# A graph and mixture-of-experts block on one core: second norm and router moved into the attention's steps, one shared-expert chunk moved behind the experts, expert weights requested behind the token table

## The chip, the cores and the metric

The kernel runs on one NeuronCore of one Trainium2 chip. The core has a matrix engine (TensorE, PE in the profile; its weight loads are PEld), a vector engine (VectorE, DVE), an activation engine (ScalarE, ACT), GpSimd (POOL) and a sync engine (SP) that issues DMAs; ACT and POOL can issue DMAs too. Each engine works through its own stream of instructions in order and waits for the others on semaphores. The metric is the device time of one execution in microseconds (us), the median of several runs.

## The reference, cut to what matters

The input is a graph of 1250 nodes with 512 features and 21250 edges. Four layers follow each other, each added to its input and each fed with a layer norm of it:

```python
x = x + attention(norm(x), edges)        # 8 heads of 32; exp(q.k), weighted by edge counts, normalised
                                         # per receiver; two 512-wide layers with relu; x_norm + out
x = x + moe(norm(x))                     # router: softmax over 64 experts, top 6; capacity 234 tokens;
                                         # gated experts of 256; plus 2 shared experts / 2
x = x + messages(norm(x), edges, attr)   # per edge relu([h[src], attr] W1 + b1) W2 + b2, summed per node,
                                         # a GRU cell, batch norm; h + bn
x = x + kan(norm(x))                     # two layers of cubic splines and silu
```

In the second layer each token goes to its six best experts. Its place inside an expert is its rank among the tokens that chose that expert, in token order; a token whose rank is 234 or more is dropped there. So routing a tile of tokens needs the counts of all tiles before it, and the first expert can start only when every token has been placed.

## The kernel before

Nodes are padded to 1280 and lie in `NT` = 10 tiles of 128 (`xr` keeps their features on chip, `hT` the normed features transposed). Wide matmuls go by `CHUNKS` of 512, 512 and 256 nodes: tiles 0 to 3, 4 to 7, 8 and 9. Everything is float32 but for masks. The program is unrolled. A planner puts the instructions of each engine in order: earlier lines of the program go first where two are ready by its own estimate; `tc.issue_after(ins)` holds a block's instructions behind `ins` on the same engine. A pool of tiles that takes over the memory of a closed pool waits for that whole pool, unless it was opened with `reuse_waits="tile"`, when each tile waits for those alone whose place it takes.

Stages, with times of the profiled execution:

- *Norm, projections and edge counts* (to 166 us).
- *Attention's steps* (166 to 385 us). There are 60 steps: 3 chunks of receivers, 2 halves of the heads, 10 tiles of senders. `scores` (L348) makes two PSUM tiles `ps` of two banks each, out of three that rotate; ACT turns them into `ex` (L358), DVE into `wt` (L360); `weighted` (L366) multiplies two steps later. `normalised` closes a half, `output` (L386) a chunk: its two dense layers are emitted in the middle of the next chunk's first half, and behind the steps for the last chunk. [...]
- *Second norm, routing and shared experts* (385 to 560 us). `layernorm` (L139) over all ten tiles, with the normed rows written to the table `xtab` in DRAM by POOL; then routing in two groups of `RG` = 5 tiles (L493 to L558): logits, softmax, the six best, one-hot `hot`, its sum `sel`, the counts before each token through two small matmuls (`pc`), the copy `slot`, the place `tat`, and 30 scatters by POOL of (token, weight) pairs into the table `tokt`. Behind it the experts are ranked by load (L566 to L591), and the shared experts run over the three chunks (L594 to L633): hidden layer `pg`, `pu`, `g`, `sT`, then `py` added into `xr`. In the last chunk SP reads the table back (`tokb`, L608) and two matmuls sort it into `tok`, `gate` and `goal`. Weights of router, shared experts and W1 came by ACT's queue long before.
- *Experts* (560 to 1085 us). 64 experts, 28 of them with two parts of 128 and 112 rows. `load` (L645) has SP request 1.5 MB of weights into one of four buffers; `rows` gathers tokens from `xtab` by POOL; `result` adds weighted rows by POOL into one of two accumulators `acc` in DRAM. The first four loads wait for nothing but the ranking.
- *Behind the experts* (1085 to 1168 us). The 20 parts of `acc` are read and added to `xr` (L742 to L746), the third norm runs in groups of two tiles, each tile is multiplied by W1 (L765) and stored in the table `ptab` (L769).
- *Messages, GRU, splines* (to the end). POOL gathers rows of `ptab` per edge, so it starts when all of the table is stored.

Of the kernel before, what the change touches and what calls it, by code (L numbers as in the profile page):

```python
# [74 lines left out]
def gnn_ffn_kernel(ctx: ExitStack, tc: tile.TileContext, a: dict, out: bass.AP):  # L75
# [63 lines left out]
    def layernorm(work, psum, each=None, pt_bufs=None, group=NT, residual=False):  # L139


        st = small.tile([P, NT, 6], F32, name="st")
        mv = small.tile([P, NT, 2], F32, name="mv")
        rs = small.tile([P, NT], F32, name="rs")
        for t0 in range(0, NT, group):
            ts = slice(t0, t0 + group)
            for t in range(t0, t0 + group):
                nc.vector.bn_stats(st[:, t], xr[:, t])
                nc.vector.bn_aggr(mv[:, t], st[:, t])
            nc.vector.tensor_scalar(rs[:, ts], mv[:, ts, 1], EPS, None, op0=OP.add)  # L150
            nc.scalar.activation(rs[:, ts], rs[:, ts], AF.Sqrt)
            nc.vector.reciprocal(rs[:, ts], rs[:, ts])
            for t in range(t0, t0 + group):
                h = work.tile([P, D], F32, name="h")
                nc.vector.tensor_scalar(h, xr[:, t], mv[:, t, 0:1], rs[:, t:t + 1],
                                        op0=OP.subtract, op1=OP.mult)
                if each:
                    each(t, h)
                pt = psum.tile([P, DC, P], F32, name="pt", bufs=pt_bufs)
                for c in range(DC):  # L160
                    nc.tensor.transpose(pt[:, c], h[:, c * P:(c + 1) * P], ident)  # L161
                nc.scalar.activation(hT[:, :, t * P:(t + 1) * P], pt, AF.Copy)
        if residual:
            up = small.tile([P, NT], F32, name="up")
            nc.vector.tensor_scalar(up, rs, 1.0, None, op0=OP.add)
            down = small.tile([P, NT], F32, name="down")
            nc.vector.tensor_mul(down, rs, mv[:, :, 0])
            for t in range(NT):
                nc.vector.tensor_scalar(xr[:, t], xr[:, t], up[:, t:t + 1], down[:, t:t + 1],
                                        op0=OP.mult, op1=OP.subtract)  # L170
# [6 lines left out]

    until_moe = ExitStack()
    shared = until_moe.enter_context(tc.tile_pool(name="shared", bufs=1))
    rw = shared.tile([P, DC, NE], F32, name="rw")  # L180
    rb = shared.tile([P, NE], F32, name="rb")
    sg = shared.tile([P, 2, DC, 2 * FF], F32, name="sg")
    sd = shared.tile([P, 2 * FF // P, D], F32, name="sd")
# [5 lines left out]
    zero = shared.tile([P, D], F32, name="zero")  # L189
# [4 lines left out]
    with tc.tile_pool(name="gat", bufs=1) as gw:  # L194
# [13 lines left out]
        with tc.tile_pool(name="gat_a", bufs=3) as work, \  # L208
# [9 lines left out]
            st = keep.tile([P, NT, 6], F32, name="st")  # L218
            mv = keep.tile([P, NT, 2], F32, name="mv")
            rs = keep.tile([P, NT], F32, name="rs")  # L220
            down = keep.tile([P, NT], F32, name="down")
            up = keep.tile([P, NT], F32, name="up")

            def norm(t0):

                ts = slice(t0, t0 + 2)
                for t in range(t0, t0 + 2):
                    nc.vector.bn_stats(st[:, t], xr[:, t])
                    nc.vector.bn_aggr(mv[:, t], st[:, t])
                nc.vector.tensor_scalar(rs[:, ts], mv[:, ts, 1], EPS, None, op0=OP.add)  # L230
                nc.scalar.activation(rs[:, ts], rs[:, ts], AF.Sqrt)
                nc.vector.reciprocal(rs[:, ts], rs[:, ts])
                nc.vector.scalar_tensor_tensor(down[:, ts], mv[:, ts, 0], -1.0, rs[:, ts], op0=OP.mult,
                                               op1=OP.mult)
                nc.vector.tensor_scalar(up[:, ts], rs[:, ts], 1.0, None, op0=OP.add)
                for t in range(t0, t0 + 2):
                    h = work.tile([P, D], F32, name="h", bufs=2)
                    nc.scalar.activation(h, xr[:, t], AF.Identity, bias=down[:, t:t + 1],
                                         scale=rs[:, t:t + 1])
                    pt = psum.tile([P, DC, P], F32, name="pt")  # L240
                    for c in range(DC):
                        nc.tensor.transpose(pt[:, c], h[:, c * P:(c + 1) * P], ident)
                    nc.scalar.activation(hT[:, :, t * P:(t + 1) * P], pt, AF.Copy)
                    nc.scalar.activation(xr[:, t], xr[:, t], AF.Identity, bias=down[:, t:t + 1],
                                         scale=up[:, t:t + 1])
# [20 lines left out]
            for n0, n in CHUNKS:  # L266
                others += [lambda t=t: norm(t) for t in range(n0 // P, (n0 + n) // P, 2)]
# [6 lines left out]
            for b in range(NT):  # L274
# [20 lines left out]
                if b in (3, 4, 5, 6):  # L295
                    with tc.issue_after(cc.ins):
                        if b == 3:
                            nc.scalar.dma_start(out=rw, in_=a["router"].rearrange("(c p) e -> p c e", p=P))
                            nc.scalar.dma_start(out=rb, in_=row(R_RB, NE))
                        elif b < 6:  # L300
                            nc.scalar.dma_start(out=sg[:, b - 4],
                                                in_=a["shared_in"][b - 4].rearrange("(c p) f -> p c f", p=P))
                        else:
                            nc.scalar.dma_start(out=sd, in_=a["shared_out"].rearrange("(c p) d -> p c d", p=P))
# [37 lines left out]

        with tc.tile_pool(name="gat_e", bufs=3) as work, \
                tc.tile_pool(name="gat_o", bufs=2) as owork, \
                tc.tile_pool(name="gat_s", bufs=3, space=PSUM) as psum, \
# [63 lines left out]
            ready, done, acc, aggT = [], None, None, None  # L409
            for i in range(len(steps) + 2):  # L410
# [10 lines left out]
                if b == NT // 2 and half == 0 and done:  # L421
                    output(*done)
                    done = None
                if b == NT - 1:
# [3 lines left out]
            output(*done)  # L428


    until_edges = ExitStack()
    mgw = until_edges.enter_context(tc.tile_pool(name="msg_w", bufs=1, side="right"))
    w1 = mgw.tile([P, DC, D], F32, name="w1")
    nc.scalar.dma_start(out=w1, in_=a["W1"][:D].rearrange("(c p) f -> p c f", p=P))
    b1 = mgw.tile([P, D], F32, name="b1")
    nc.scalar.dma_start(out=b1, in_=row(R_B1, D))


    with tc.tile_pool(name="moe", bufs=1) as mw, tc.tile_pool(name="moe_w", bufs=4) as ew:
        tri = mw.tile([P, P], BF, name="tri")  # L440
        nc.gpsimd.affine_select(out=tri, in_=ones, pattern=[[1, P]], base=0, channel_multiplier=-1,
                                compare_op=OP.is_gt, fill=0.0)
        onesb = mw.tile([P, P], BF, name="onesb")
        nc.vector.memset(onesb, 1.0)
        ei = mw.tile([P, NE], I32, name="ei")
# [760 lines left out]
```

## Time and profile before

| | |
|---|---|
| median of 3 runs | 2061.09 us (2058.55 to 2063.27) |
| profiled execution, its own time | 2108.56 us |
| its span | 2106.7 us |
| mean granted TensorE clock | 0.959 |
| TensorE busy | 1920.8 us, 91% |
| VectorE busy | 1036.7 us, 49% |
| ScalarE busy | 722.7 us, 34% |
| GpSimd busy | 468.1 us, 22% |
| DMA | 250.56 MB, mean 119 GB/s |

The profile is one execution. A row of the order of time gives the start, the time taken, the engine, the line, the operation with the tile it writes and those it reads, how many were merged, and in square brackets how long the engine had been idle before it and what ended that wait. A row of stretches gives the busy time of each engine in a part of the span. "issue" and "remote" mark waits that the recorded semaphores don't explain. The profiled execution took 47.5 us longer than the median.

### The profile page before, as it was taken

The page shows a single profiled execution, that of the slowest core. Times are in us where ns is not written, and L with a number is a line of the kernel's source. Part 1 is how long each engine was busy: PE and PEld are TensorE (multiplying, and loading weights), DVE is VectorE, ACT ScalarE, POOL GpSimd, SP SyncE. Part 2 cuts the span into 40 slices and gives each one's busy share as a digit, 9 for nine tenths or more (in the row PEclk, how much of TensorE's full clock was granted, in tenths as well). Part 3 has the DMA queues.
Part 4 walks back from the last instruction along what each step waited for, and adds up shares of the span by engine and source line. Part 5 has one row for each costly group of instructions (what it writes and reads, how often), then busy time and mean ns, then how long its engine had stood idle before and what let it go on. Part 6 is the DMA issues. An engine that isn't in the chain of part 4 may idle for free. (4 is left out here: it accounts for less than half of the span.)

```text
span 2106.7 us, 20943 instructions
## 1 busy us (share of the span) xinstructions
PE 1920.8 (91%) x7761; PEld 1033.7 (49%) x7761; DVE 1036.7 (49%) x1690; ACT 722.7 (34%) x1114; POOL 468.1 (22%) x436
## 2 busy tenths in 40 slices
PE   6999999784999999999957899999999968889889
PEld 4573224441666666666523233333444756465454
DVE  8667786550211111111125455551122269999995
ACT  3216554200022121121211234341112178777773
POOL 0000000165144444444420556650000000000000
PEclk9999999896999999999988999999999988999999
DMA  6010000231299999999972677770100020000000
GB/s 234 24 40 2 1 1 1 75 98 26 59 280 272 279 280 272 274 269 276 281 225 84 210 234 240 245 238 16 53 23 0 1 90 1 1 10 11 10 1 19
DMA packets 68945, 250.56 MB, mean 119 GB/s; under 512 B 11760, under 2 KB 14448, under 8 KB 59860
## 3 DMA queue, kind: packets, MB, share of 16 engines
q1 hardware_dynamic: 24658, 137.60, 18.7%
q0 software_dynamic: 36240, 92.89, 17.3%
q10 hardware_dynamic: 7922, 18.50, 2.6%
q8 instruction: 67, 1.10, 0.2%
q14 instruction: 58, 0.48, 0.1%
HBM read 211.98 MB, written 36.96 MB: 118 GB/s over the span
## 5 line engine op out<-in xcount | busy, mean ns | idle before, releaser
L718 POOL DMA_INDIRECT acc<-y,goal x92 | 144.5, 1570 | 215.2 <-ACT y L716 120.4
L173 POOL DMA_INDIRECT hg<-ptab,srci x167 | 158.4, 949 | 144.0 <-DVE m L802 53.9
L1069 PE MATMUL pk<-basis,w1s 128*128 128x256 f32 x640 | 158.6, 401 | 29.6 <-DVE basis L1051 29.6
L800 PE MATMUL pm<-w1e,eat 128*128 128x512 f32 x334 | 169.7, 623 | 6.5 <-DVE m L802 5.6
L713 PE MATMUL py<-w,gT 128*128 128x512 f32 x368 | 169.5, 595 | 2.0 <-ACT gT L706 1.4
L1091 PE MATMUL py<-w2s,basis 128*128 128x512 f32 x320 | 148.0, 626 | 21.2 <-DVE basis L1051 21.2
L1069 PEld LDWEIGHTS pk<-basis,w1s 128*128 128x128 f32 x640 | 124.1, 199 | 64.8 <-DVE basis L1051 46.1
L802 DVE TENSOR_TENSOR m<-pm,hg 128x1024 f32<-128x1024 f32 x84 | 102.3, 1218 | 103.6 <-PE pm L800 83.2
L803 ACT ACTIVATE m<-m 128x1024 f32<-128x1024 f32 x84 | 88.3, 1051 | 164.7 <-DVE m L802 148.8
L1028 DVE SCALAR_TENSOR_TENSOR cube<-held,knots,sq 128x512 f32<-128x512 f32 x180 | 136.0, 757 | 1.7 <-ACT sq L1024 1.7
L716 ACT ACTIVATE y<-py,gate 128x512 f32<-128x512 f32 (+1 forms) x92 | 63.3, 688 | 206.5 <-PE py L713 197.7
L1024 ACT ACTIVATE sq<-held,negk 128x512 f32<-128x512 f32 x180 | 126.1, 710 | 20.6 <-DVE held L1016 20.6
L360 DVE SCALAR_TENSOR_TENSOR wt<-ex,cnts 128x1024 f32<-128x1024 f32 (+1 forms) x120 | 118.7, 1039 | 23.0 <-ACT ex L358 22.9
L693 PE MATMUL pg<-w,xT 128*128 128x512 f32 x288 | 129.5, 592 | 0.2 <-issue 0.2
L358 ACT ACTIVATE ex<-ps 128x1024 f32<-128x1024 f32 (+1 forms) x120 | 100.6, 881 | 77.3 <-PE ps L353 64.6
L173 POOL DMA_INDIRECT xg<-xtab,tok x92 | 90.2, 981 | 127.6 <-PE pt L689 44.4
L1091 PEld LDWEIGHTS py<-w2s,basis 128*128 128x128 f32 x320 | 64.0, 201 | 103.4 <-issue 76.8
L800 PEld LDWEIGHTS pm<-w1e,eat 128*128 128x128 f32 x334 | 55.5, 190 | 102.6 <-issue 89.6
L682 DVE TENSOR_TENSOR gT<-gx,pu 128x480 f32<-128x480 f32 x28 | 18.3, 654 | 177.0 <-PE pu L679 177.0
L713 PEld LDWEIGHTS py<-w,gT 128*128 128x128 f32 x368 | 65.6, 186 | 76.0 <-issue 71.9
L679 PE MATMUL pg<-xT,w 128*128 128x240 f32 x448 | 98.1, 372 | 2.9
L697 DVE TENSOR_TENSOR gs<-gs,pg 128x256 f32<-128x256 f32 x36 | 15.2, 422 | 168.6 <-ACT gs L696 168.6
(273 smaller groups left out, 3076.3 us busy)
## 6 DMA issues: line engine op xcount, KB each, us to landing
w<-in_experts SPq DMA_DIRECT2D x64, 1536.0 KB
eat<-in_edge SPq DMA_DIRECT2D x20, 512.0 KB
acc<-zero SPq DMA_DIRECT2D x22, 256.0 KB
part<-acc SPq DMA_DIRECT2D x20, 256.0 KB
w1s<-in_w1s ACTq DMA_DIRECT2D x4, 1024.0 KB
w2s<-in_w2s SPq DMA_DIRECT2D x2, 2048.0 KB
wih<-in_Wih ACTq DMA_DIRECT2D x4, 768.0 KB
whh<-in_Whh ACTq DMA_DIRECT2D x4, 768.0 KB
```

Source lines behind the costliest of these rows:

```text
L173: nc.gpsimd.indirect_dma_start(out=dst, out_offset=None, in_=table, in_offset=IndirectOffsetOnAxis(ap=at, axis=0))
L358: nc.scalar.activation(ex[:, :, :n], p[:, :, :n], AF.Exp, scale=DK ** -0.5)
L360: nc.vector.scalar_tensor_tensor(wt[:, :, :n], ex[:, :, :n], HUGE, cnts[:, b, None, n0:n0 + n].to_broadcast([P, 2, n]), op0=OP.min, op1=OP ...
L693: nc.tensor.matmul(ph[:m], xT[:, c, :m], self.w[:, c:2 * DC:DC], start=c == 0, stop=c == DC - 1)
L713: nc.tensor.matmul(py[:m], self.gT[:, f, at:at + m], self.w[:, k:k + 2].rearrange("p a b -> p (a b)"), start=f == 0, stop=f == 1)
L718: nc.gpsimd.indirect_dma_start(out=next(turn), out_offset=IndirectOffsetOnAxis(ap=goal[:m, self.r, h:h + 1], axis=0), in_=y[:m, j], in_off ...
L800: nc.tensor.matmul(pm[:, i], eat_t, w1e, start=True, stop=True)
L802: nc.vector.tensor_add(m[:, :k], pm[:, :k], hg[:, :k])
L1024: nc.scalar.activation(self.sq[k], self.x, AF.Square, bias=negk[:, k:k + 1])
L1028: nc.vector.scalar_tensor_tensor(self.cube[k], self.x, knots[:, k:k + 1], self.sq.pop(k), op0=OP.subtract, op1=OP.mult)
L1069: nc.tensor.matmul(pk[o], w[:, o * P:(o + 1) * P], b[:, c], start=half == 0 and g == 8 and c == 0, stop=half == 1 and g == 7 and c == 1)
L1091: nc.tensor.matmul(py[m], b[:, c, m * P:(m + 1) * P], w, start=g == 8 and c == 0, stop=g == 7 and c == 1)
```

## The change

Seven edits belong together.

1. The two norms in the code become one class `Norm`, whose `parts` is a generator: it yields behind each two tiles of statistics and behind each tile. ACT can make `h` (`scalar=True`) and did so in the first norm already.
2. Routing becomes a generator `route(t0, n, ...)`, defined ahead of the attention. Its constants are made there. It runs by chunk: tiles 0 to 3, 4 to 7, 8 and 9. Behind a chunk's `output`, each following step of the attention emits one part; what is left runs behind the last step. Its PSUM tiles are `ps` tiles of the scores.
3. Router weights stay where they were in time; the shared experts' weights are requested by SP behind the attention's steps, into memory that the attention's tiles leave (`reuse_waits="tile"`), no longer by ACT in the count stage.
4. The shared experts become a function. Chunk 0 runs ahead of the table, chunk 2 behind it, chunk 1 behind the experts.
5. The first expert's weights are held behind the request for `tokb` (`loads` starts with it).
6. W1 and `b1` are requested behind the tenth expert's weights by SP, no longer by ACT ahead of the routing.
7. Behind the experts, pools wait by tile; parts, third norm, W1 and stores go by pairs of tiles in the order 0, 2, 8, 4, 6, with the third norm's residual update last. `rT` is cleared by DVE, no longer by POOL.

```diff
@@ Norm
-    def layernorm(work, psum, each=None, pt_bufs=None, group=NT, residual=False):
+    class Norm:
+        def parts(self, t0, n, work, psum, name="pt", each=None, scalar=False, bufs=None, pt_bufs=None):
...
+                if (t - t0) % 2:
+                    yield
...
+                if scalar:
+                    nc.scalar.activation(h, xr[:, t], AF.Identity, bias=self.down[:, t:t + 1],
+                                         scale=rs[:, t:t + 1])
...
+                yield
@@ count stage
-                if b in (3, 4, 5, 6):
+                if b == 3:
...
-                            nc.scalar.dma_start(out=sg[:, b - 4],
-                                                in_=a["shared_in"][b - 4].rearrange("(c p) f -> p c f", p=P))
@@ routing, ahead of the attention's steps
+        def route(t0, n, work, psum):
+            yield from norm2.parts(t0, n, work, psum, name="ps", scalar=True, bufs=2, each=lambda t, h: nc.gpsimd.dma_start(
+                out=xtab[1 + t * P:1 + (t + 1) * P], in_=h))
...
+            pl = psum.tile([P, n, NE], F32, name="ps")
...
+            nc.scalar.activation(pr, pr, AF.Exp)
+            yield
...
+            with nc.allow_low_precision(reason="zeros and ones"):
+                nc.vector.tensor_reduce(sel[:, ts], hot.rearrange("p t k e -> p t e k"), AX.X, OP.add)
+            yield
+            pc = psum.tile([P, n, NE], F32, name="ps")
...
+            slot, u = new("slot", NE), new("u", NE)
+            nc.vector.tensor_copy(slot, pc)
...
@@ attention's steps
-            ready, done, acc, aggT = [], None, None, None
+            ready, done, acc, aggT, parts = [], None, None, None, iter(())
...
                 if b == NT // 2 and half == 0 and done:
                     output(*done)
+                    parts = chain(parts, route(done[0] // P, done[1] // P, rwork, psum))
                     done = None
+                else:
+                    next(parts, None)
...
             output(*done)
+            for _ in chain(parts, route(done[0] // P, done[1] // P, rwork, psum)):
+                pass
@@ shared experts' weights
+    shared = until_moe.enter_context(tc.tile_pool(name="shared", bufs=1, reuse_waits="tile"))
...
+    for i in range(2):
+        nc.sync.dma_start(out=sg[:, i], in_=a["shared_in"][i].rearrange("(c p) f -> p c f", p=P))
+    nc.sync.dma_start(out=sd, in_=a["shared_out"].rearrange("(c p) d -> p c d", p=P))
@@ table and shared experts
-            for n0, n in CHUNKS:
-                sT = keep.tile([P, 2 * FF // P, 512], F32, name="sT")
...
+            last = shared_experts(*CHUNKS[0], keep, psum, psum1)
+            tokb = keep.tile([P, P, 2], F32, name="tokb")
+            landed = nc.sync.dma_start(out=tokb, in_=tokt[:NPOS].rearrange("(q p) o -> q p o", p=P))
...
+            shared_experts(*CHUNKS[2], keep, psum, psum1)
-            loads, turn = [], cycle(accs)
+            loads, turn = [landed], cycle(accs)
...
-                        with tc.issue_after(loads[-1].ins) if i else nullcontext():
+                        with tc.issue_after(loads[-1].ins) if loads else nullcontext():
                             experts[i].load()
...
+            with tc.issue_after(loads[10].ins):
+                nc.sync.dma_start(out=w1, in_=a["W1"][:D].rearrange("(c p) f -> p c f", p=P))
+                nc.sync.dma_start(out=b1, in_=row(R_B1, D))
@@ behind the experts
+    psum = finishing.enter_context(tc.tile_pool(name="msg_p", bufs=2, space=PSUM))
+    psum1 = finishing.enter_context(tc.tile_pool(name="msg_q", bufs=1, space=PSUM))
+    shared_experts(*CHUNKS[1], late, psum1, psum1)
+    norm3 = Norm()
+    for t0 in (0, 2, 8, 4, 6):
+        for t in (t0, t0 + 1):
+            for i, acc in enumerate(accs):
+                part = ywork.tile([P, D], F32, name=f"part{i}")
+                nc.sync.dma_start(out=part, in_=acc[t * P:(t + 1) * P])
+                nc.vector.tensor_add(xr[:, t], xr[:, t], part)
+        norm3.group(t0, 2, lwork, psum)
+        for t in (t0, t0 + 1):
+            pp = psum.tile([P, D], F32, name="pp")
...
+            nc.sync.dma_start(out=ptab[t * P:(t + 1) * P], in_=pv)
+    norm3.residual(0, NT)
...
-            nc.gpsimd.memset(rT, 0.0)
+            nc.vector.memset(rT, 0.0)
```

The new function for the shared experts, called with `psum` of two buffers ahead of the experts and with `psum1` of one buffer for both behind them:

```python
    def shared_experts(n0, n, work, psum, psum1):
        sT = work.tile([P, 2 * FF // P, 512], F32, name="sT")
        for f in range(2 * FF // P):
            pg = psum.tile([P, 512], F32, name="pg")
            pu = psum1.tile([P, 512], F32, name="pu")
            for i, p in ((0, pg), (1, pu)):
                for c in range(DC):
                    nc.tensor.matmul(p[:, :n], sg[:, i, c, f * P:(f + 1) * P], hT[:, c, n0:n0 + n],
                                     start=c == 0, stop=c == DC - 1)
            g = work.tile([P, 512], F32, name="g", bufs=2)
            nc.scalar.activation(g[:, :n], pg[:, :n], AF.Silu)
            nc.vector.tensor_mul(sT[:, f, :n], g[:, :n], pu[:, :n])
        for t in range(n // P):
            po = psum.tile([P, D], F32, name="py")
            for f in range(2 * FF // P):
                last = nc.tensor.matmul(po, sT[:, f, t * P:(t + 1) * P], sd[:, f], start=f == 0,
                                        stop=f == 2 * FF // P - 1)
            xs = xr[:, n0 // P + t]
            nc.vector.scalar_tensor_tensor(xs, po, 0.5, xs, op0=OP.mult, op1=OP.add)
        return last
```

## The prediction

> **What bounds the kernel now.** I read the page first, then the busy time by stretches, then the order of time around the widest holes of TensorE.
>
> The page's busy row; the busy time by stretches (columns: stretch, length, busy PE, PEld, DVE, ACT, POOL, granted clock, DMA share, GB/s):
>
> ```profile
> PE 1920.8 (91%) x7761; PEld 1033.7 (49%) x7761; DVE 1036.7 (49%) x1690; ACT 722.7 (34%) x1114; POOL 468.1 (22%) x436
> ...
> 271.40:325.65 54.25, 51.69 (x481) 14.82 (x480) 49.60 (x51) 34.33 (x44) 0.00 (x0) 1.00 0.00 1
> 325.65:346.80 21.15, 21.15 (x52) 8.87 (x48) 4.98 (x8) 2.94 (x5) 0.00 (x0) 1.00 0.00 1
> 346.80:370.40 23.60, 23.08 (x321) 10.19 (x320) 21.02 (x33) 14.26 (x27) 0.00 (x0) 1.00 0.01 2
> ...
> 385.20:559.90 174.70, 131.52 (x422) 73.01 (x423) 60.36 (x151) 19.74 (x30) 72.20 (x79) 0.84 0.22 65
> 559.90:1085.20 525.30, 520.24 (x1993) 338.53 (x1991) 90.13 (x157) 102.46 (x191) 229.25 (x179) 1.00 0.91 266
> 1085.20:1168.30 83.10, 44.96 (x129) 22.29 (x129) 43.52 (x93) 8.65 (x19) 10.77 (x7) 0.78 0.40 128
> ```
>
> TensorE sets the pace nearly everywhere, so the change is worth what it takes out of TensorE's holes: 43 us of 174.7 between the attention and the experts, 38 of 83.1 behind the experts. But in the attention's steps VectorE is almost as full: 49.6 of 54.25, 21.0 of 23.6. The order of time shows the holes:
>
> ```profile
> 392.02 3.65 PE L161 MATMUL pt<-ident,h 128*128 128x128 f32 x16 [6.83 <-DVE h L155]
> ...
> 512.10 6.24 PE L601 MATMUL pu<-hT,sg 128*128 128x512 f32 x8 [28.38 <-issue]
> ...
> 1116.87 3.80 PE L161 MATMUL pt<-ident,h 128*128 128x128 f32 x16 [31.71 <-DVE h L155]
> ...
> 489.58 0.60 ACT L604 ACTIVATE g<-pg 128x512 f32<-128x512 f32 x1 [27.27 <-remote]
> ...
> 511.35 0.69 DVE L605 TENSOR_TENSOR sT<-g,pu 128x512 f32<-128x512 f32 x1 [37.87 <-issue]
> ...
> 509.33 0.96 POOL L553 DMA_INDIRECT tokt<-entry,tat  x1 [0.30 <-issue]
> ...
> 513.14 0.33 SPq L608 DMA_DIRECT2D tokb<-tokt  x1
> ```
>
> The hole at 484 to 512 is odd: the matmuls that ACT and DVE want were issued 21 us and more before, no dependence is late, and it began with four weight transfers (456 to 478, DMA share 0.94) and ended with the scatters. Lost by it: 5.0 us at 468, 28.4 at 484, and 3.3 and 2.8 in two groups that took 6.75 and 6.24 us instead of 3.43: 39.6. Without it the table (requested at 513.1, some 2.5 us to land) would hold up TensorE by 2.5, so 37 us are at stake.
>
> [...]
>
> **The change, part by part.**
> 1. *Routing in the attention (tiles 0 to 3, 4 to 7).* A group of five costs DVE: `sel` 3.46; `hot`, `hu`, `pos` 2.16, 2.16, 2.14; eight passes over 320 elements at 0.49; max and index 2.3; `before` 1.1; small ones. For four tiles, 4/5 of what goes by elements: 2.8 + 5.2 + 3.1 + 1.7 + 0.9 + 2.0 small = 15.6 us (the statistics ran in the steps before, too). Tiles 0 to 3 fall into 271.4 to 325.65: 49.6 + 15.6 = 65.2 against 54.25: +11. Tiles 4 to 7 fall into 346.8 to 370.4: 21.0 + 15.6 = 36.6 against 23.6, +13, of which the last two parts (1.7 and 2.4) come behind the last `wt`: +9. TensorE's share (transposes 4 x 0.43, router 32 at 0.12 to 0.19, counting 0.5: some 6 a group) and ACT's (`h` and `hT` 8 x 0.6, two table switches) lie beside that. ACT's square root and exponential wait for DVE with the next steps' `ex` queued behind them, and TensorE's `weighted` matmuls wait for those through `wt`; the lookahead of two steps (5.9 or 3.3 us) should cover that. POOL has nothing else in these steps, so its 8 table writes and 48 scatters there delay nobody. The routing's 12 `ps` tiles come out of the three that the scores rotate in: 5 us for bubbles. Sum +25. From +12 (the two steps of lookahead swallow DVE's lag, TensorE's own 12 remain) to +45 (all 31 serial, more than a us for each `ps` tile).
> 2. *Between attention and experts.* Before: 174.7. After the last output matmul: output adds 2.5, statistics 1.6, scale 1.1, `h` 1.5, transposes and `hT` 2.0, router 1.2, softmax 2.5, max and index 0.9, `topf` and `hot` 1.6, `sel` 1.4, counts and `slot` 1.2: about 17 us of a chain of two tiles. TensorE waits all of it, since the new PSUM pools take the banks of `ps`, whose last reader is `slot` (from 10, if only single banks are waited for, to 22). Then ranking 1, shared chunk 0 of 12 x 3.43 = 41.2, table 0.6, chunk 2 of 8 x 1.73 + 2 x 3.43 = 20.6. Sum 80.4, -94.3.
>    Covers: the last 36 scatters at 1.265 (24 from about 396, 12 from 432) end near 447, the table lands near 453, chunk 0 covers to 470. The first weights, 5.8 us each at 270 GB/s, land from 459; they are wanted at 491. With the cover gone each would cost its whole delay. Shared weights, 3 MB on SP's queue behind the last scores (390): 12 us, wanted at 427; nothing but the table is queued behind them.
> 3. *Experts.* 525.3 as before; W1 and `b1`, 1.3 MB or 5 us of DMA, hide in a share of 0.91 over 525 us, the weights being four deep.
> 4. *Behind the experts.* Before, from 1085.2 to the last W1 matmul at 1158.1: 72.9. After: branch and PSUM release 3.3 (ACT restarts at 1088.6), chunk 1 41.2, ten tiles of 0.43 + 3.44 = 38.7, and single-buffered `py`, three waits of 1.0: 86.2. +13. The parts' loads and adds (1092 to 1112) hide behind chunk 1. DVE's `rT` memset (4.4 on POOL), too: DVE has 43.5 of 83.
>
> Sum: 25 - 94 + 13 = -56, that is 2052 against the profiled execution's own 2108.56 (span 2106.7). That execution is 47.5 above the median, 2061.09. The hole of 37 explains most of it, and signals 1.5 to 9 us late in the messages, beside POOL's gathers, could be the rest; so I take it that timed runs have no such hole. Then 37 of the 56 aren't there to be had: 2061 - 19 = **2042**.
>
> **Rivals.**
> *A. The hole is in every run* and goes, the weights being behind the table now. For it: 27 us of waits that the profile shows as such. Against it: the 47.5. Time 2061 - 56 = 2005.
> *B. The `ps` ring paces the attention; slower.* Each of 12 routing tiles holds one of three `ps` until DVE or ACT reads it in its turn behind two `wt` (2.36) and a part (1.2): 3.6 us a handover instead of the 0.4 counted. For it, from the groups of the attention's stretch (shapes kept apart), the idle time of the scores' weight loads, most of it for an `ex` that must free its `ps`:
>
> ```profile
> L353 PEld LDWEIGHTS ps<-QT,KT 32*128 32x128 f32 x480 | 19.6, 183 | 45.3 <-ACT ex L358 36.4 <-issue 5.1 <-PEq L312 1.6
> ```
>
> Against it: TensorE itself hardly waited (51.69 of 54.25 busy), and `wt` runs two steps ahead. 12 x 3.6 - 5 = +38: 2080. It decides from 2 us each.
> *C. The end gives it back*: chunk 1 comes on top of, not into, the 31.7 us hole (a branch, or an order in which norm tiles stand ahead of it): another 20 us, 2062.
> *D. The hole moves*: shared weights now cross the scatters of tiles 4 to 7 where DVE's chain is bare, 20 us or more: 2065.
>
> **How the numbers follow.** A measurement of this kernel can tell 0.2% (4 us) from no change. My forecast 55% (2025 to 2057), A 17%, B 18%, C 5%, D 5%. Faster by over 0.2%: 53 of the 55 and A, and a little of B: 72%. Within 0.2%: C and edges: 8%. Slower: 20%. The range of 8 in 10, 1998 to 2075, takes all of the forecast, two thirds of A, C, D and a third of B; the forecast's own is 2025 to 2057.
>
> **What would show it.** Attention's end (last output matmul, 385.2) near 410, DVE full in the steps; a wait of some 17 before the first shared matmul, ended by `slot`; first expert transposes near 491; no weight transfer across scatters, and no wait of 27 on ACT; the 31.7 us hole gone, message matmuls 93 to 96 us behind the last expert instead of 83. Wrong, if the attention grows by over 45, if profile and median still lie 47 apart (then the hole wasn't the difference), or if the experts take over 530.

## The result and the profile after

The changed kernel takes 2065.9 us (median of 16 runs, 2061.97 to 2069.62) beside 2060.2 us (2057.37 to 2066.13, 16 runs) for the kernel before, run beside it: ratio 1.0025, 95% interval 1.0017 to 1.0033. It is slower by 0.25%, where 2042 and faster had been forecast. Its profiled execution has a span of 2064.1 us and a granted clock of 0.975, so this one does stand for its median.

The page's busy row of the changed kernel:

```profile
PE 1923.1 (93%) x7761; PEld 1030.8 (50%) x7761; DVE 1036.9 (50%) x1722; ACT 738.7 (36%) x1135; POOL 461.7 (22%) x435
```

The work of TensorE and VectorE is the same to 2.3 us (1920.8 and 1036.7 before); what has changed is where it lies. The busy time by stretches, cut at the changed kernel's own borders (columns as before: stretch, length, busy PE, PEld, DVE, ACT, POOL, clock, DMA share, GB/s):

```profile
270.40:345.50 75.10, 65.17 (x538) 22.56 (x538) 64.35 (x92) 42.34 (x56) 13.24 (x15) 0.93 0.05 15
345.50:367.40 21.90, 21.90 (x60) 9.22 (x64) 5.60 (x9) 2.92 (x6) 13.64 (x14) 1.00 0.02 1
367.40:404.20 36.80, 29.59 (x333) 15.51 (x326) 28.24 (x62) 21.86 (x38) 2.23 (x4) 0.95 0.20 68
404.20:424.65 20.45, 16.24 (x69) 8.47 (x68) 8.95 (x17) 3.94 (x7) 8.61 (x9) 0.85 0.27 87
424.65:503.54 78.89, 70.21 (x215) 39.69 (x216) 23.37 (x68) 9.71 (x16) 32.50 (x34) 0.94 0.28 102
503.54:1028.80 525.26, 520.25 (x1993) 338.52 (x1991) 90.11 (x157) 102.46 (x191) 228.94 (x179) 1.00 0.92 268
1028.80:1118.80 90.00, 83.99 (x217) 37.89 (x216) 44.07 (x101) 18.50 (x27) 1.55 (x1) 0.98 0.33 103
1118.80:1132.50 13.70, 7.14 (x13) 2.82 (x12) 7.77 (x10) 1.26 (x2) 7.59 (x8) 0.75 0.54 157
```

Read against the rows of before: the stage between the attention and the experts is 78.9 us instead of 174.7, and the experts take 525.3 as they did. But the attention now ends at 424.6 instead of 385.2. The rows of tiles 0 to 3 and 4 to 7 show where. Those of before were 54.25 us, with VectorE busy for 49.6 and TensorE for 51.7, and 23.6 us, with 21.0 and 23.1. Now they are 75.1 us with 64.4 and 65.2, and 36.8 us with 28.2 and 29.6: both engines have more work there, over stretches that have grown by more than that work, so both stand idle for longer than before. And from the last expert matmul to the last W1 matmul it is 90.0 us instead of 72.9, with 13.7 more to the first message sum (`ps`), 103.7 in all; in the profile of before that is 1170.3 - 1085.2 = 85.1.

The order of time has waits in the steps and at the end:

```profile
298.56 3.79 PE L391 MATMUL ps<-rw,hT 128*128 128x64 f32 x32
303.75 0.42 ACT L398 ACTIVATE pr<-pr 128x256 f32<-128x256 f32 x1 [5.17 <-DVE pr L397]
316.16 0.62 PE L485 MATMUL acc<-wt,V 128*32 128x512 f32 x2 [2.84 <-DVE wt L473]
402.75 0.20 PE L429 MATMUL ps<-sel,tri 128*128 128x64 bf16 x1 [1.69 <-DVE sel L424]
404.14 0.21 PE L430 MATMUL ps<-before,onesb 128*128 128x64 bf16 x1 [1.13 <-DVE before L428]
413.07 4.71 PE L506 MATMUL ps<-aggT,wa 128*128 128x256 f32 x12 [4.21 <-DVE aggT L496]
...
1031.38 5.37 PE L569 MATMUL pg<-hT,sg 128*128 128x512 f32 x8 [2.57 <-PEq L748]
1036.84 0.60 ACT L572 ACTIVATE g<-pg 128x512 f32<-128x512 f32 x1 [7.25 <-PE pg L569]
1043.19 1.29 DVE L767 TENSOR_TENSOR xr<-xr,part 128x512 f32<-128x512 f32 x2 [0.91 <-DMA part<-acc]
1045.01 0.67 DVE L573 TENSOR_TENSOR sT<-g,pu 128x512 f32<-128x512 f32 x1
1045.73 3.70 PE L569 MATMUL pu<-hT,sg 128*128 128x512 f32 x8 [2.12 <-DVE sT L573]
1119.58 0.32 SPq L775 DMA_DIRECT2D ptab<-pv  x1
1122.29 0.33 SPq L787 DMA_DIRECT2D w1e<-in_W  x1
1125.38 7.17 PE L818 MATMUL pm<-w1e,eat 128*128 128x512 f32 x10 [6.56 <-DMA w1e<-in_W]
```

ACT stands 5 us before the softmax's exponential with the next `ex` queued behind it. That looks like a price of its order, but the scores for that `ex` are themselves late: TensorE makes them behind the router's 3.79 us of matmuls. `weighted` matmuls wait for a `wt` that VectorE makes behind the long `sel` (2.7 us), and in tiles 4 to 7 TensorE stands 1.7 and 1.1 us before the small count matmuls with `weighted` behind them, and later waits 4.2 us for `aggT`. At the end, chunk 1's first eight matmuls take 5.37 us instead of the usual 3.43. Its second `pu` waits 2.1 us for the first `sT`. That one had its `g` since 1037.4, but VectorE came to it only at 1045.0, behind adds of `part` that wait for their DMA. And the lower part of W1 (`w1e`) is requested behind the last store of the table. That last wait looks dear and is not: POOL can gather from the table only from 1122.8, and before took 5 us from there to the first message `m`. That `m` comes 10.3 us behind the last W1 matmul instead of 8.9, so the late request costs 1.5.

### The profile page after: what moved, and what is told of

Read it like the earlier page. It is cut to its first block, busy times and chain, and to the rows that moved or that the text cites. A ratio compares the mean times of both kernels' runs of the same rounds, so it can differ in the third digit from the quotient of the medians.

```text
span 2064.1 us, 20996 instructions
## 1 busy us (share of the span) xinstructions
PE 1923.1 (93%) x7761; PEld 1030.8 (50%) x7761; DVE 1036.9 (50%) x1722; ACT 738.7 (36%) x1135; POOL 461.7 (22%) x435
## 5 line engine op out<-in xcount | busy, mean ns | idle before, releaser
L471 ACT ACTIVATE ex<-ps 128x1024 f32<-128x1024 f32 (+1 forms) x120 | 101.1, 881 | 86.7 <-PE ps L466 65.2
## 6 DMA issues: line engine op xcount, KB each, us to landing
w2s<-in_w2s SPq DMA_DIRECT2D x2, 2048.0 KB, 10.9
```

## Two kinds of chip

One thing has to be said ahead of the experiments, since their numbers can't be read without it. The kernel before took 2060 and 2061.5 us on two occasions (the first is that of the result) and 2101 to 2108 us on four, on three chips of which one came up twice. The first profile is of the second kind, though the timed runs given with it are of the first; on which chip that profile was taken is not on record. No chip was seen in both ways, so it is not shown whether the chip makes the difference or the occasion. Below, "quiet" is a chip on which before took about 2061 at the time, "late" one on which it took 2101 or more, and a time is set beside that of before on the same occasion. Where runs of different chips are compared, it is by these ratios, and the text says so.

**before_again, before3, before4, before5**: the kernel before, unaltered, for more profiles.

> The kernel before, unaltered, for a second profile. If the hole of 37 us at 484 to 512 us belonged to the one recorded execution: no wait of TensorE over 6 us between 440 and 515, the experts' first transposes near 522, own time near 2060. If the hole is in every execution (rival A): again 25 to 40 us lost there, experts near 560, and a profiled time near 2108.

> The kernel before, unaltered, for a profile on a chip on which its time is near 2061. If what the timed runs lack is the hole alone: no signal over 1.5 us late, last output matmul near 384, experts near 521, last expert matmul near 1046, first message sum near 1131, end near 2060. Otherwise it shows which other stage is shorter than in the first profile.

> The kernel before, unaltered, for a profile. On a chip where its time is near 2061: no signal over 1.5 us late, last output matmul near 384, experts near 521, last expert matmul near 1046, first message sum near 1131, end near 2060; if another stage is shorter too, it shows here. On a chip where its time is near 2105: as the first profile, experts near 560.

> The kernel before, unaltered, for a profile. Where its time is near 2061: no signal over 1.5 us late, last output matmul near 384, experts near 521, last expert matmul near 1046, first message sum near 1131; if another stage is shorter too, it shows here. Where its time is near 2105: experts between 551 and 563, as in four profiles.

All four fell on late chips: 2099.7, 2108.8, 2102.1 and 2102.1 us, with medians of before there of 2102.1 (36 runs), 2108.1 (15), 2101.5 (15) and 2101.5 (7). So profile and timed runs agree on each. The experts start at 551.0, 562.5, 553.3 and 553.5, near the first profile's 559.9: the hole is in every profile taken on a late chip, and not a chance of one execution. There is no profile of before on a quiet chip; that it has no hole there is concluded from its time, 40 us shorter.

**before_late**: edit 5 alone, on a late chip.

```diff
-                    nc.sync.dma_start(out=tokb, in_=tokt[:NPOS]...)
+                    landed = nc.sync.dma_start(out=tokb, in_=tokt[:NPOS]...)
...
-            loads, turn = [], cycle(accs)
+            loads, turn = [landed], cycle(accs)
...
-                        with tc.issue_after(loads[-1].ins) if i else nullcontext():
+                        with tc.issue_after(loads[-1].ins) if loads else nullcontext():
...
```

> Edit 5 alone on the kernel before: the first expert's weights are requested behind the table. If the hole was in one execution only, there is nothing to win: 2056 to 2064 us, ratio 0.998 to 1.002 (weights are requested near 515 and wanted near 522: a few us late at most, 2065). Rival A, hole in every run and made by weights crossing the scatters: about 2025 us, ratio 0.983.

2100.6 us beside 2102.1, ratio 0.9994 (0.9982 to 1.0005). Its order of time at the hole:

```profile
508.51 0.33 SPq L608 DMA_DIRECT2D tokb<-tokt  x1
512.44 4.16 SPq L650 DMA_DIRECT2D w<-in_experts  x4
512.56 0.69 DVE L605 TENSOR_TENSOR sT<-g,pu 128x512 f32<-128x512 f32 x1 [39.92 <-remote]
513.30 5.22 PE L601 MATMUL pu<-hT,sg 128*128 128x512 f32 x8 [33.48 <-DVE sT L605]
```

The hole is there, 33.5 us of TensorE, with no expert weight requested before 512. VectorE waits 39.9 us for a signal that the trace can't place ("remote"), until 8 us behind the start of the last scatter (504.7). So the weights don't make the hole. What it shares with its like in every late profile is the row of small scatters that POOL issues at that time. In the two profiles of the changed kernel from quiet chips no wait of 0.4 us or more is marked remote, with the same scatters.

**after_again, after3**: the changed kernel on a quiet and on a late chip.

> The changed kernel, unaltered, beside the kernel before on one chip. Where the kernel before takes about 2102 us here (a chip on which signals come late while POOL scatters): the hole of 37 to 40 us is in before and some 20 to 30 of it in the changed kernel (in the steps during tiles 0 to 3's scatters and at tiles 8 and 9), so 2085 to 2095, ratio 0.992 to 0.997. Where before takes about 2060: 2066, ratio 1.0025, with no late signal in either. If the chip made no difference, the ratio would be 1.0025 in both.

> The changed kernel once more. Where before takes 2097 us or more (signals late beside the scatters): the changed kernel pays for its scatters in the steps some 15 to 20 us and at tiles 8 and 9 some 10, before pays 40 and more, so 2090 to 2095, ratio 0.991 to 0.996. Where before takes about 2061: 2065, ratio 1.002.

Quiet: 2064.8 us beside 2061.5, ratio 1.0020 (1.0013 to 1.0027). Late: 2101.5 beside 2101.5, ratio 0.9998 (0.9989 to 1.0007). On the late chip the changed kernel doesn't escape: the scatters of tiles 0 to 3, which now run from 332 to about 363 beside the steps, meet ACT and VectorE there:

```profile
347.79 0.60 ACT L471 ACTIVATE ex<-ps 128x512 f32<-128x512 f32 x1 [5.65 <-remote]
352.01 0.63 PE L485 MATMUL acc<-wt,ones 128*32 128x256 f32 x1 [0.78 <-issue]
359.76 0.59 PE L485 MATMUL acc<-wt,ones 128*32 128x256 f32 x1 [0.82 <-issue]
366.12 1.08 ACT L471 ACTIVATE ex<-ps 128x512 f32<-128x512 f32 x2 [14.91 <-PE ps L506]
```

TensorE is hit too: from 352 to 366 us its matmuls start 1.4 us apart, and no recorded signal explains the waits between them. So the trace doesn't tell whether it is signals or instructions that come late; "late" below says no more than that.

The attention ends at 445.9 instead of 423.2, the stage behind it takes 88.1 us instead of 78.7 and the part behind the first message sum 938.5 instead of 930.0: 23 + 9 + 8.5, less 1.5 behind the experts, make the 39 us between the two spans. Before loses 40 between the two kinds of chip, by its late profiles most of it in its hole.

## The experiments on the parts

**after_bare, bare2**: all routing behind the steps.

```diff
-                    parts = chain(parts, route(done[0] // P, done[1] // P, rwork, psum))
                     done = None
-                else:
-                    next(parts, None)
...
-            for _ in chain(parts, route(done[0] // P, done[1] // P, rwork, psum)):
-                pass
+            for n0, n in CHUNKS:
+                for _ in route(n0 // P, n // P, rwork, psum):
+                    pass
```

> The changed kernel with all routing emitted behind the attention's steps. Theory that routing in the steps costs 39 us there but starts the scatters early enough to be worth it: last output matmul back near 385 us, scatters from about 431 to 511 one after the other, table near 515, chunk 2 of 20.6 behind it, experts near 537: about 2099 us. Rival (the 39 us are pure loss, the scatters are covered anyway): experts start at 503 or before, 2066 us or less.

> The changed kernel with all routing behind the steps, on a chip without late signals. Theory that routing in the steps is worth more by starting the scatters early than the 38 us it costs there: steps end near 385, scatters run to 510, experts near 535, about 2095 us, ratio 1.016. Rival (pure loss): experts at 503 or before, 2066 or less, ratio 1.002 or less.

Both on late chips: 2116.2 us beside 2102.1, ratio 1.0053 (1.0034 to 1.0072), and 2109.4 beside 2108.1, ratio 1.0017 (0.9997 to 1.0037). The attention ends at 392.8 and 392.5, and the experts start at 550.1 and 540.3, where the changed kernel on a late chip has 445.9 and 534.0. The ratios less the changed kernel's 0.9998, all three from different chips, put routing in the steps at a gain of 12 and 4 us, not the some 30 that were expected; the smaller of the two is within the intervals. So on late chips it is no pure loss, and not much of a gain. What it is worth on a quiet chip, for which the expectation was meant, stays open.

**after_c1front**: chunk 1 back ahead of the experts, on a late chip.

```diff
-            last = shared_experts(*CHUNKS[0], keep, psum, psum1)
+            shared_experts(*CHUNKS[0], keep, psum, psum1)
+            last = shared_experts(*CHUNKS[1], keep, psum, psum1)
...
-    shared_experts(*CHUNKS[1], late, psum1, psum1)
```

> The changed kernel with shared chunk 1 back ahead of the experts (behind chunk 0). Theory that chunk 1 fills holes behind the experts: the experts start 41 us later (near 545), from the last expert matmul to the last W1 matmul 73 us instead of 90, sum +24: about 2090 us. Rival C (the end gives all back): 2066, as the changed kernel.

2114.4 us beside 2102.1, ratio 1.0059 (1.0041 to 1.0077): by the ratios, from two chips, 0.6% or 13 us worse than the changed kernel, half of the 24 expected. The front grows by 37 us (experts at 571.0 instead of 534.0). Behind the experts it is 63.2 us to the last W1 matmul instead of 88.9. That is less than the 72.9 of before: the new arrangement of that stage, in pairs of tiles, closes by itself some 10 us of the hole that chunk 1 was counted to fill, so chunk 1's 41 us cost 26 there.

**after_sel**: the mask `sel` by one comparison; 2.4 us less of VectorE for four tiles.

```diff
-            with nc.allow_low_precision(reason="zeros and ones"):
-                nc.vector.tensor_reduce(sel[:, ts], hot.rearrange("p t k e -> p t e k"), AX.X, OP.add)
+            nc.vector.tensor_tensor(sel[:, ts], pr, top[:, :, TOPK - 1:TOPK].to_broadcast([P, n, NE]), OP.is_ge)
+            if t0 + n == NT:
+                nc.vector.tensor_scalar(sel[:, NT - 1], sel[:, NT - 1], real, None, op0=OP.mult)
```

> The changed kernel with the choice mask made by one comparison with the sixth best probability (0.4 us) in place of the sum over the one-hot form (2.8 us for four tiles): 2.4 us less of VectorE in each of two groups, 1 less behind the steps. Theory that in the steps VectorE's work is the price, us for us: 4 to 6 us faster than the changed kernel. Rival that waits in the order of ACT and TensorE are the price: 0 to 2 faster.

Quiet chip: 2058.4 us beside the changed kernel's 2064.8, so 6.4 faster, and ratio 0.9987 (0.9975 to 0.9999) to before. The two stretches of steps with routing, first in the changed kernel (after_again), then here:

```profile
272.30:344.80 72.50, 62.97 (x529) 21.58 (x530) 63.43 (x92) 42.26 (x56) 12.51 (x15) 0.95 0.05 16
367.20:402.70 35.50, 27.91 (x323) 14.45 (x316) 27.58 (x60) 21.20 (x37) 2.23 (x4) 0.99 0.21 72
```

```profile
272.40:341.60 69.20, 61.22 (x529) 21.32 (x523) 60.70 (x92) 42.22 (x56) 12.77 (x14) 0.98 0.05 16
363.90:397.30 33.40, 28.26 (x332) 14.70 (x324) 25.45 (x65) 21.21 (x38) 2.23 (x4) 1.00 0.14 49
```

VectorE's work falls by 2.7 and 2.1 us, the stretches by 3.3 and 2.1, and the attention ends 6.1 earlier with TensorE's instructions the same. So at the margin, by these 4.8 us of VectorE and 5.4 us of steps, a microsecond of VectorE in these steps is about a microsecond of the kernel, and TensorE's own added work alone doesn't set their length. (The forecast had VectorE as the limit too and would give the same slope. How much longer the steps are than VectorE's work is another question, on which the next run bears.)

**after_hold**: the same work, the exponential and the count matmuls one step later. Both are held behind the step's last `ex` on ACT and last `weighted` matmul on TensorE (kept in `marks`), so that the planner can't sort them forward again.

```diff
-            nc.scalar.activation(pr, pr, AF.Exp)
+            yield
+            with tc.issue_after(marks["ACT"]):
+                nc.scalar.activation(pr, pr, AF.Exp)
...
+            yield
+            pc = psum.tile([P, n, NE], F32, name="ps")
+            with tc.issue_after(marks["PE"]):
                 for t in range(n):
                     nc.tensor.matmul(pc[:, t], tri, sel[:, t0 + t], start=True, stop=False)
...
```

> The changed kernel with the softmax's exponential put one step later on ACT, behind that step's ex, and the count matmuls one step later on TensorE, behind that step's weighted matmuls; the same work. Rival that waits in the order of ACT and TensorE are the price of the steps beyond VectorE's work: 6 to 9 us faster than the changed kernel (5.2 for the exponential in tiles 0 to 3, 2 to 4 for the count matmuls). Theory that VectorE's work alone is the price: 0 to 2 faster.

Quiet chip: the attention ends at 418.2 instead of 423.2, 5.0 earlier (0.6 of it from ahead of the steps with routing), but the kernel takes 2065.2 us beside 2064.8. In tiles 0 to 3 the held exponential gains nothing. ACT now goes to the `ex` first, and waits for it about as long:

```profile
298.74 3.79 PE L391 MATMUL ps<-rw,hT 128*128 128x64 f32 x32
303.63 1.94 ACT L476 ACTIVATE ex<-ps 128x1024 f32<-128x1024 f32 x2 [4.87 <-PE ps L471]
```

That stretch is 2 us shorter, and 2.5 are won at the end of the steps, where `aggT` comes earlier. The gain is lost 45 us later. The first scatter for tiles 4 to 7 in the changed kernel (after_again) and here, and the order of time where the gain goes:

```profile
412.26 1.00 POOL L448 DMA_INDIRECT tokt<-entry,tat  x1 [30.49 <-DVE tat L445]
```

```profile
412.40 1.00 POOL L453 DMA_INDIRECT tokt<-entry,tat  x1 [32.46 <-DVE tat L450]
...
462.83 0.22 DVE L622 CAST order<-pt 1x65 int32<-1x65 f32 x1 [14.65 <-DMA tokt<-entry,tat]
463.69 2.93 PE L574 MATMUL pu<-hT,sg 128*128 128x512 f32 x3 [6.01 <-DVE sT L578]
```

The copy of the experts' order, a row of 65 numbers, lies in a pool that takes over the memory of the routing's scratch (`gat_r`), from which the scatters read. So it waits 14.65 us, for the last scatter; `sT`, whose `g` was done at 458.3, is queued behind it on VectorE and starts at 462.97, and the next `pu` behind that. In the changed kernel the same copy waits 9.5 us (9.6 in the result's profile) but costs TensorE only 0.8 to 1.0. The holds have shortened the steps but not the way to the places `tat`: the last 36 scatters begin at the same time (412.26 and 412.40) and end at the same time (the last is issued at 459.11 and 459.16). So the work between has 5 us more to wait, and the matmuls behind the wait take 6.2 us instead of 3.7: the experts start 2.7 us later than in the changed kernel. By this trace the last scatter, through the copy, holds up the experts' start, and not the steps.

**after_best**: the two edits together, and behind the experts the third norm's square roots held behind chunk 1's last silu, two `py` buffers, and `w1e` loaded with W1.

```diff
+            with tc.issue_after(behind) if behind else nullcontext():
                 nc.scalar.activation(rs[:, ts], rs[:, ts], AF.Sqrt)
...
-            po = psum.tile([P, D], F32, name="py")
+            po = psum.tile([P, D], F32, name="py", bufs=py_bufs)
...
-    shared_experts(*CHUNKS[1], late, psum1, psum1)
+    _, silu = shared_experts(*CHUNKS[1], late, psum1, psum1, 2)
...
-        norm3.group(t0, 2, lwork, psum)
+        norm3.group(t0, 2, lwork, psum, behind=silu.ins)
...
+                nc.sync.dma_start(out=w1e, in_=a["W1"][D:])
```

> Both of these together, and behind the experts: the third norm's square roots behind the last silu of chunk 1, two py buffers, W1's lower part loaded with W1. Sum of 5, 6, and 4 to 6 behind the experts (2.4 for the waits on sT, some 3 for py and pm): 14 to 18 us faster than the changed kernel, near 2050 where before takes 2060. If the three overlap or the steps stay bound by the same chain: 6 to 10 faster.

Quiet chip: 2061.1 us, 3.7 under the changed kernel, ratio 0.9994 (0.9983 to 1.0005) to before. The attention ends 8.9 earlier, the experts start only 3.6 earlier: the copy of the order again (14.6 us, 5.9 of TensorE). Behind the experts the edits gave 0.6 to the last W1 matmul and 1.8 from there to the first message sum, not the 4 to 6 expected: TensorE had work for all but 6 of those 90 us. The second `pu` still waits 1.6 us there, with no table change between the silus:

```profile
1041.45 3.70 PE L577 MATMUL pu<-hT,sg 128*128 128x512 f32 x8 [1.63 <-DVE sT L581]
```

The three edits together are also 2.7 us slower than after_sel alone, whose experts start at 495.6, against 498.3 here. On the quiet chip the cheaper mask by itself is the fastest kernel here, and the only one whose ratio to before has its interval below 1.

**hold_order, hold_order2** (after_hold) **and best2, best3, best4** (after_best) with the order kept elsewhere:

```diff
-            order = mw.tile([1, NE + 1], I32, name="order")
+            order = rt.tile([1, NE + 1], I32, name="order")
```

> The kernel with the exponential and the count matmuls one step later, and the experts' order kept in the memory of the routing's tiles instead of where the attention's routing scratch was. Theory that the 5 us won in the steps were lost because the copy of the order waits for the last scatter with the sT of chunk 0 queued behind it on VectorE: no wait of 6 us before the fourth pu, experts' first transposes near 498 instead of 504.6, 2058 to 2060 us where before takes 2061.5, ratio 0.998 to 0.9995. Rival that the last scatter bounds the stage by the table anyway: 2065, ratio 1.002.

> All of it: mask by comparison, exponential and count matmuls later, order elsewhere, and the edits behind the experts. Theory as above: 6 us under the 2061 of the same without the order's place: 2053 to 2056 us where before takes 2061.5, ratio 0.996 to 0.9975; experts near 492. Rival: 2061.

> Exponential and count matmuls one step later and the experts' order kept elsewhere. Where before takes about 2061, theory that the copy of the order, waiting for the scatters ahead of sT, was what lost the 5 us won in the steps: experts near 498, 2058 to 2060, ratio 0.998 to 0.9995. Rival that the table bounds the stage: 2065, ratio 1.002. Where before takes about 2105: 2087 as measured.

> Mask by comparison, exponential and count matmuls later, order elsewhere, edits behind the experts. Where before takes about 2061: 2053 to 2056, ratio 0.996 to 0.9975, experts near 492; rival 2061, ratio 0.9995. Where before takes about 2105: 2076 as measured.

> Mask by comparison, exponential and count matmuls later, order elsewhere, edits behind the experts. Where before takes about 2061: if the copy of the order, waiting for the last scatter ahead of sT, was what held up the same kernel without the order's new place (2061.1), then no wait of 6 us before the fourth pu, experts near 492 instead of 498.3, 2053 to 2056, ratio 0.996 to 0.9975; rival that the table bounds the stage anyway: 2061, ratio 0.9995. Where before takes about 2105: 2076, as measured twice.

All five fell on late chips. hold_order: 2086.9 us beside 2108.1 and 2084.1 beside 2101.5, ratios 0.9896 (0.9858 to 0.9933) and 0.9920 (0.9904 to 0.9937). best: 2076.0, 2076.3 and 2076.0, ratios 0.9851 (0.9814 to 0.9888), 0.9877 (0.9857 to 0.9896) and 0.9870 (0.9841 to 0.9900). There it is well ahead of before, and on the one late chip on which the changed kernel ran (2101.5) of that, too. best4's order of time:

```profile
449.56 0.29 DVE L441 COPY slot<-ps 128x128 f32<-128x128 f32 x1 [9.92 <-remote]
457.17 0.22 DVE L625 CAST order<-pt 1x65 int32<-1x65 f32 x1 [2.70 <-PE pt L623]
```

The copy no longer waits for the scatters, but for the matmul that makes it. In its place a wait marked remote holds `slot` for 9.9 us beside the scatters of tiles 4 to 7. So on these chips the stage between is no shorter (89.6 us in hold_order2, 88.1 in the changed kernel); the 17 us that hold_order2 has over after3 on the same chip come from the steps, which end at 428.2 instead of 445.9. There other work now lies beside the first scatters, which begin at 339.9 instead of 332.4; that this is the reason is not shown, and no run on a late chip has the holds without the order's new place. What that place is worth on a quiet chip, which these runs were to show, stays open.

## Why the prediction was wrong

By its own steps, on quiet chips, for which its 2042 was meant (the numbers of before are those of its first profile):

| step | predicted | measured |
|---|---|---|
| 1 routing in the steps | +25 | +39.4 (385.2 to 424.6) |
| 2 between attention and experts | 174.7 to 80.4 | 78.9 |
| 3 experts | 525.3 | 525.3 |
| 4 behind the experts | 72.9 to 86.2, +13 | 90.0, +17; to the first message sum +18.6 |
| hole in timed runs | none | none on quiet chips, by their times; whole on late ones |

**Step 1 failed, by 14 us of the 24.** Its work was right: 15.6 us of VectorE for four tiles, and VectorE's busy time grew by 64.4 - 49.6 = 14.8. What failed is the overlap. "49.6 + 15.6 = 65.2 against 54.25: +11", and its like for tiles 4 to 7, filled VectorE's idle time with routing and left nothing over, and "the lookahead of two steps (5.9 or 3.3 us) should cover that" put the waits between the engines at nothing. The stretch took 75.1 us, 20.9 more and not 11, with VectorE idle in 10.8 of it where it had been idle in 4.6; its waits for `ex` grew from 3.8 to 7.6 us in all. TensorE had been fuller still, with 51.7 of 54.25, and its busy time grew by 13.5, at a mean clock of 0.93 instead of 1.00, where some 6 had been counted as lying beside.

Over all steps VectorE's work grew by 14.8 + 7.2 + 6.3 = 28.3 of the 39.4 us, and after_sel shows that such work is paid about us for us (5.4 us of steps for 4.8 of VectorE). Of the other 11, after_hold won 4.4 by a new order of the same instructions; how the rest divides is not shown. In the program each `wt` needs an `ex`, each `ex` a `ps`, and each `weighted` matmul a `wt`, so the three engines work in turn; that this turn is what kept the idle time from being filled is a reading of the waits. The range had most of it in its upper bound of +45. The forecast's signs were an attention that ends near 410 and a full VectorE: it ended at 424.6, with VectorE 86% busy.

**Step 2 held** in its sum, though not in each part. TensorE did not wait some 17 us for `slot`: chunk 0's first `pu` ran from 435.7, 11 us behind the attention's end and ahead of `slot` (442.4). And one cover was thinner than said. The scatters were to end near 447 and chunk 0 to cover to 470; they ended at 461.5, since tiles 4 to 7's places come only at 413, near the end of the steps, and the copy of the order, which no step had, ties VectorE to them. In the changed kernel that costs 1 us; by the traces it took the 5 of after_hold and most of after_best's gain.

**Step 4 was mis-sized**, by 4 us to the last W1 matmul and by 5.6 to the first message sum. The five pairs of norm and W1 took 41.3 instead of 38.7 us (8.26 each: 1.04, 7.13 and small waits), chunk 1's first matmuls 1.9 more, and two waits for `sT` 2.4; 1.5 is the late request for `w1e`. The waits for `sT` come from VectorE's order, with adds of `part` ahead of `sT`. ACT's changes of tables for the third norm's square roots (seven loads of 1.28 us from 1037 to 1070) had little to do with them: after_best has none between the silus and still waits 1.6. Less than was counted went to the start of chunk 1 (2.6 instead of 3.3) and to `py`.

**The hole.** That the timed runs of the result had none was right. That the profiled execution was the exception was wrong: the hole is in each profile from a late chip, with the time to match. Of the 39.6 us laid to it, 6.1 were two slow groups of eight matmuls: while they ran (473.5 to 480.1 and 512.1 to 518.3 of the first profile) the granted clock was 0.53 and 0.58. The rest of the miss, 24 - 14 - 5.6 + 1.5 (step 2), is some 5 us. The experts fit, so it lies in the base, the 37 us that were taken off the gain or stages of before that are shorter still without late signals. The kernel before was never profiled on a quiet chip, so it can't be divided further.

**The rivals.** A (in every run, and goes) was half right on the hole and wrong on its going: on a late chip the changed kernel loses as much elsewhere. That weights across the scatters cause it fell with before_late. B had the attention as the place, but would have it 25 + 38 = 63 us longer, not 39, and its mechanism is not seen: over the first stretch the scores' weight loads waited for `ex` 8.0 us in 8 waits and those of the routing's own `ps` tiles some 4, against 10.9 in 15 for the scores before, where B needs 3.6 for each of 12 tiles. So the `ps` ring was not the pace. C was not so: by the ratios chunk 1's move is worth 13 us on a late chip. D was not seen: no shared weight transfer stood out, and what held `slot` in late runs was a wait marked remote. That the times of C and D, 2062 and 2065, come nearest to the measured 2066 is chance.

## What to carry to other kernels

When work is put into a pipeline of steps in which one or two engines are almost full, don't count on their idle time to take it. Here VectorE had 4.6 us idle in 54 and TensorE 2.6; 14.8 us more of VectorE made the stretch 20.9 longer. After each saving ask what is late next: after_hold ended the steps 5 us earlier, but the places that the scatters need came no earlier, and nothing was won. Look for small instructions that wait for memory rather than data, like the copy of the order, one line of 65 numbers, which waited 14.65 us in after_hold. And before a hole in a profile is priced, see whether the timed runs have it, on the chip on which they will run.

## What was not expected of the hardware

The same program took about 2061 us on two occasions and 2101 to 2108 on four. On the latter, waits of up to 40 us are marked remote, and they stand beside POOL's rows of indirect DMAs (8-byte scatters 1.27 us apart, and later the gathers of the messages); others, TensorE's among them, have no recorded end at all. In three late profiles of before (the first, before_again, before4) TensorE waited 32 to 33 us in the hole; the changed kernel lost 23 in the steps, 9 behind them and 8.5 in the messages. That this is because of the indirect DMAs is read from where the waits lie in time. No run took the scatters away, and why it happens on some chips or occasions alone is open.
